# A four-layer graph network: scatter-adding the last layer's expert rows into the output, and moving weights and products at three earlier borders

## The chip, the cores and the metric

The kernel runs on one core of a Trainium2 chip. The metric is device time in microseconds (us) of one execution, the median of the runs; lower is better.

## The reference

A graph of 1250 nodes with 512 features and 21250 edges (sorted by target) passes through four layers. Each layer adds a graph convolution and a linear attention of the normalized features, then a routed feed-forward step:

```python
xn = _layernorm(x)
x = x + gnn(xn, edges) + mix(xn)
x = x + ffn(_layernorm(x))
```

- Layer 0: three GATv2 convolutions, one after another (`m = leaky_relu(xl[src] + xr[dst] + ef)`, softmax of `m @ att` over the edges of a target, weighted sum of `xl[src]`), with `xl = x @ Wl[k]`, `xr = x @ Wr[k]`; a linear attention; 8 experts that choose their nodes.
- Layer 1: two GAT convolutions, a global linear attention (`q`, `k`, `v` by three weights), 8 routed experts and 2 shared ones.
- Layer 2: a convolution with combined bases, linear attention, 10 experts.
- Layer 3: GCN, linear attention, and 32 experts with a capacity, the part that the diff touches most:

```python
probs = softmax(x_flat @ Wg); vals, idx = top_k(probs, 2)
vals = vals / vals.sum(-1)
a = idx.reshape(BTK)                          # BTK = 2500 choices
pos = rank of each choice among those of its expert
keep = pos < C                                # C = 98
dest = where(keep, a * C + pos, N * C)
buf = zeros((N * C, D)).at[dest].set(x_flat[token], mode='drop')
h = relu(einsum('ncd,ndh->nch', buf, W1) + b1)
o = einsum('nch,nhd->ncd', h, W2) + b2
y = segment_sum(o[dest] * (vals * keep), token)
y = where(contrib <= 1e-12, x_flat, y)        # a node that no expert kept
```

All data are float32.

## The kernel before

One class, `Net`, holds the program. Nodes lie in NT = 10 tiles of 128 (the last has 98 rows); `self.x` stays in SBUF. Small helpers do the recurring steps: `weight` (L141, a 1 MB weight by SyncE), `gather` (L231) and `scatter` (L239), both indirect DMAs issued by GpSimd, `evac` (L134, PSUM to SBUF, in turn on ScalarE and VectorE), `feat` (L179, a transposed product), `add_scaled` (L1811). The order on each engine is the program's order as the Tile framework schedules it; `manual_schedule` holds one engine to the written order.

Layer 0's convolutions are `gatv2_fast`. Edges are worked off in groups of four tiles: gathered left rows `xl` (table `tl`, by GpSimd), target fields (`fields`: a broadcast row `nb` and edge attributes, loaded two groups ahead), one-hot matrices (`onehot`, ScalarE), right products of the block (L1286, L1287), scores (`logits`, VectorE, L1299 and L1302), and sums by target (L1353). As a block's targets finish, their nodes' tables for the *next* convolution are made: `gat_tables` (L1154) gives ten closures for a tile, four matmuls with `wl` and `left` (adds the score column, stores to `tl`), then four with `wr` and `right` (splits the value in two, stores to `tr`). They are queued in `late` and run one at a time. `prepare` loads vectors and weights for the convolution after that, from the seventh step on. At the end of a convolution the queues are emptied, and the next starts with `fields(0)`, three `load`s, `fields(1)`, `onehot(0)`.

From layer 0 to layer 1: after the last expert of layer 0 (`layer0_ffn`), 20 gathers bring the expert rows back to their nodes (L231, L1811), the tiles are normalized and transposed, and `global_attention` starts with the weight `wk`; `wv` is loaded when the code comes to it. Between its products stand the steps that count edges per pair of node blocks (L711 matmuls on stored one-hot blocks, `ohb<-oht`, L688).

From layer 2 to layer 3: `tail_steps` gives `need(t)`, which fetches the last two expert rows of a node tile (pipelined over tiles), adds and normalizes. `layer3_attn` calls it tile by tile, beside GCN products (L171). `linear_attention_steps` loads its three weights itself.

Layer 3's feed-forward step, `layer3_ffn`: the router's products and top 2; ranks by matmuls; each node's row is scattered to its places `dest` in the table `routed_in` (20 scatters). The biases b2 and rows of unrouted nodes are added to `self.x`. Then for each of 32 experts: load 98 rows `xe` (ScalarE's queue), transpose (L3164), first product (L179) with ReLU on ScalarE, second product (L3173) into a PSUM bank `y`, evacuate to `o`, store to `routed_out` (ScalarE's queue); two weights are loaded ahead, up to 11 in flight. After the last expert:

```python
for t in range(NT):
    for j in range(2):
        g = tmp.tile([128, D], F32, tag="g", name="g", bufs=4)
        self.gather(g, self.rout[:, :], getI[:, t, j:j + 1])
        self.add_scaled(t, g, w0[:, t, j:j + 1])
    r = rows(t)
    nc.sync.dma_start(self.out[t * 128:t * 128 + r, :], self.x[:r, t, :])
```

Of the kernel before, what the change touches and what calls it, by code (L numbers as in the profile page):

```python
# [16 lines left out]
I32 = mybir.dt.int32  # L17
# [40 lines left out]
class Net:  # L58
# [79 lines left out]
    def weight(self, src, k, n):  # L138

        w = self.wp.tile([128, k, n], F32, tag="w", name="w")  # L140
        self.nc.sync.dma_start(w, src.rearrange("(k p) n -> p k n", p=128))  # L141
        return w
# [591 lines left out]
    def linear_attention_steps(self, xn, xT, w_qkv, w_out, b_out, qscale, finish, added=None,  # L734
                               need=None):
# [14 lines left out]
        with self.tc.tile_pool(name="la", bufs=1) as p, \  # L750
                self.tc.tile_pool(name="latmp", bufs=2) as tmp:
            wk = self.weight(w_qkv[:, D:2 * D], 4, D)
            wv = self.weight(w_qkv[:, 2 * D:3 * D], 4, D)
# [4 lines left out]
            for half in range(2):  # L758
                if half:
                    wq = self.weight(w_qkv[:, 0:D], 4, D)  # L760
                    if qscale != 1.0:
                        nc.scalar.mul(wq, wq, qscale)
# [446 lines left out]
    def gat_layer(self, L, p, xtab, otab, big):  # L1209
# [27 lines left out]
        step = [0]  # L1237

# [16 lines left out]
        def fields(g):  # L1255
            nb = p.tile([128, GE * 128], BF16, tag="nb", name="nb", bufs=4)
            nc.sync.dma_start(nb, self.nbt[g])
            s = p.tile([128, GE * 128], F32R, tag="oh", name="oh", bufs=3)
            nc.sync.dma_start(s[BW:K].bitcast(F32),
                              self.eat[:, g * GE * 128:(g + 1) * GE * 128])  # L1260
            G.setdefault(g, {}).update(nb=nb, s=s)
# [99 lines left out]
        def finish(b):  # L1361
# [44 lines left out]
            def across():  # L1406
# [10 lines left out]
                for t in whole:  # L1417
                    for f in self.gat_tables(nxt, p, t, lambda c, t=t: X[t][:, c, :],
                                             lambda: self.bank("tab", [128, D])):
                        late.append((step[0] + 1, f))  # L1420
# [37 lines left out]
        fields(1)  # L1458
        onehot(0)
        prepared = prepare()  # L1460
        for i in range(FT + 3):
# [9 lines left out]
            if j == 2 and g + 2 < FG:  # L1471
                fields(g + 2)
            if i >= 6 and i % 3 == 0:
                next(prepared, None)
# [19 lines left out]
        bias_cur(NB - 1)  # L1494
        while edge or todo or late:
            for _ in range(2):
                if edge:
                    edge.popleft()[1]()
            for _ in range(2):
                if todo:  # L1500
                    todo.popleft()[1]()
            for _ in range(2):
                if late:
                    late.popleft()[1]()
        return nxt
# [24 lines left out]
    def layer0_ffn_to_layer1_attn(self):  # L1530
# [11 lines left out]
        with self.tc.tile_pool(name="l1a", bufs=1) as p:  # L1542
            xnT = p.tile([128, 4, NP], F32, name="xnT")
            with self.tc.tile_pool(name="l1b", bufs=1) as pb:
                xn = pb.tile([128, NT, D], F32, name="xn")
                with self.weights(), self.psum(3, 2, 3) if fast else self.psum():
                    count_pool()
                    self.counting = self.count_blocks(range(CB), True) if fast else iter(())
                    self.layer0_ffn(xn, xnT)
# [7 lines left out]
                    self.global_attention(xn, xnT, steps)  # L1557
# [91 lines left out]
    def layer0_ffn(self, xn, xnT):  # L1649
# [6 lines left out]
        with self.tc.tile_pool(name="l0f", bufs=1) as p, \  # L1656
# [126 lines left out]
            for t in range(NT):  # L1783
                for j in range(2):
                    g = tmp.tile([128, D], F32, tag="g", name="g", bufs=6)
                    self.gather(g, obuf[:, :], getI[:, t, j:j + 1])
                    self.add_scaled(t, g, G[:, t, j:j + 1])
                self.ready(t)
                self.norm_tile(t, xn[:, t, :])
                self.transpose_tile(xnT[:, :, t * 128:(t + 1) * 128], xn[:, t, :])  # L1790
                self.count(1)
            g1.close()

# [12 lines left out]

    def add_scaled(self, t, psum, gate):
# [6 lines left out]
    def global_attention(self, xn, xnT, steps):  # L1814
# [3 lines left out]
        with self.tc.tile_pool(name="ga", bufs=3) as big, \  # L1818
# [5 lines left out]
            wk = self.weight(I["L1_mix_WkT"], 4, D)  # L1824
# [20 lines left out]
            wv = self.weight(I["L1_mix_WvT"], 4, D)  # L1845
# [531 lines left out]
    def tail_steps(self, xn, xnT):  # L2377
# [22 lines left out]
        def need(t):  # L2400
            with self.tc.manual_schedule(engines={mybir.EngineType.Pool}):
                for u in range(t - n if t == 0 else t, t + 1):
                    for i, f in enumerate(steps):
                        if 0 <= u + n - i < NT:
                            f(u + n - i)
        return need
# [522 lines left out]
    def layer3_attn(self):  # L2929
        nc, I = self.nc, self.I  # L2930
        added = self.both_added()
        with self.tc.tile_pool(name="l3", bufs=1) as p:
            xnT = p.tile([128, 4, NP], F32, name="xnT")
            xn = p.tile([128, NT, D], F32, name="xn")
            need = self.tail_steps(xn, xnT)
# [12 lines left out]
            with self.tc.tile_pool(name="gcn", bufs=2) as tmp:  # L2948
# [3 lines left out]
                else:  # L2952
# [5 lines left out]
                    added)  # L2958
# [77 lines left out]
    def layer3_ffn(self):  # L3036
        nc, I = self.nc, self.I
        NE, ROWS = 32, 32 * CAP
        with self.tc.tile_pool(name="l3f", bufs=1) as p, \
# [15 lines left out]
            xn = p.tile([128, NT, D], F32, name="xn")  # L3055
# [9 lines left out]
            for t in range(NT):  # L3065
                self.norm_tile(t, xn[:, t, :])
# [19 lines left out]
            getI = p.tile([128, NT, 2], I32, name="getI")  # L3086
            G = p.tile([128, NT, NE], F32, name="G")
            with self.tc.tile_pool(name="l3r", bufs=1) as pr1:
# [35 lines left out]
                for t in range(NT):  # L3124
                    r = rows(t)
                    for j in range(2):
                        self.scatter(self.rin, putI[:r, t, j:j + 1], xn[:r, t, :], "moe")
                for j in range(2):
# [4 lines left out]
                nc.vector.tensor_scalar(dest, dest, float(ROWS - 1), None, op0=ALU.min)  # L3133
                nc.vector.tensor_copy(getI, dest)
# [7 lines left out]
                                        op=ALU.mult)  # L3142
                for j in range(2):
# [3 lines left out]
            for t in range(NT):  # L3147
# [7 lines left out]
                self.add_scaled(t, xn[:, t, :], none[:, t:t + 1])  # L3155
            for e in range(NE):
                w1, w2 = ws[2 * e], ws[2 * e + 1]
                er = slice(e * CAP, (e + 1) * CAP)
                xe = tmp.tile([CAP, D], F32, tag="xe", name="xe", bufs=3)
                nc.scalar.dma_start(xe, self.rin[er, :])  # L3160
# [14 lines left out]
                o = tmp.tile([CAP, D], F32, tag="o", name="o")  # L3175
                self.evac(o, y)
                nc.scalar.dma_start(self.rout[er, :], o)
# [4 lines left out]
            for t in range(NT):  # L3182
                for j in range(2):
                    g = tmp.tile([128, D], F32, tag="g", name="g", bufs=4)
                    self.gather(g, self.rout[:, :], getI[:, t, j:j + 1])
                    self.add_scaled(t, g, w0[:, t, j:j + 1])
                r = rows(t)
                nc.sync.dma_start(self.out[t * 128:t * 128 + r, :], self.x[:r, t, :])
# [69 lines left out]
```

## Time and profile before

| | |
|---|---|
| median of 3 runs | 4463.08 us (4459.12 to 4470.91) |
| the profiled execution | 4489.82 us, its span 4487.9 us |
| mean granted TensorE clock | 0.937 |
| instructions | 49486 |
| data moved by DMA | 647.58 MB, mean 144 GB/s |
| last stage: last matmul of an expert ends | 4443.4 us |

The profile is one execution, by the hardware profiler. Times in it are us from the span's start. PE is TensorE, PEld its weight loads, DVE VectorE, ACT ScalarE, POOL GpSimd, SP SyncE; a "q" after an engine is its sequencer or DMA queue. Groups of instructions name line, engine, operation and tile (`out<-in`), count, busy time, mean ns, and the idle time of the engine just before them with what ended most of it. The chain lists the work that ended last, followed back from the end. Stretches give the busy time of each engine in a window, with the granted clock, the mean busy share of the 16 DMA engines and what they moved. Timelines list instructions by start and duration, with the engine's idle time before each in brackets.

### The profile page before, as it was taken

Reading aid. Unit: us, or ns where it says so; the run is one execution under the profiler, and the core shown is the slowest. Engines: PE = TensorE matmul, PEld = TensorE weight load, DVE = VectorE, ACT = ScalarE, POOL = GpSimd, SP = SyncE. Lnnn points to the kernel's source line nnn. Section 1 sums busy time; section 2 is a strip of 40 time slices with the busy share of each in tenths; the row PEclk is TensorE's granted clock in tenths of the full one; section 3 lists DMA queues with packets and bytes.
Section 4 is the critical chain, followed back from the end, with each engine's and each line's share of the span. In section 5 each row is a group of like instructions: output and inputs, shape, how many; then the busy total and the mean of one; then the engine's idle time right before and its main releaser. Section 6 shows DMA issues by size and latency. Waiting matters only on the chain. (4 is left out here: it accounts for less than half of the span.)

```text
span 4487.9 us, 49486 instructions
## 1 busy us (share of the span) xinstructions
PE 3922.2 (87%) x15466; PEld 2415.7 (54%) x15466; DVE 2689.5 (60%) x6338; ACT 1622.8 (36%) x2976; POOL 1351.0 (30%) x1308
## 2 busy tenths in 40 slices
PE   5987998899788867799999999997979896898796
PEld 3434554455354434444788877563546562455474
DVE  5357895888398865523896767314584225687301
ACT  2222442344133375110464446223451232554121
POOL 2017773776466501102000000103131013675102
PEclk9988999999899988899999999999989998997798
DMA  6437664666466423402421110383002653666695
GB/s 220 159 84 211 198 199 150 198 197 193 141 179 189 145 74 108 119 17 64 146 70 42 46 35 29 143 298 128 12 27 83 233 189 119 182 200 199 225 339 181
DMA packets 283001, 647.58 MB, mean 144 GB/s; under 512 B 61673, under 2 KB 108905, under 8 KB 267322
## 3 DMA queue, kind: packets, MB, share of 16 engines
q1 hardware_dynamic: 169290, 357.13, 24.1%
q0 software_dynamic: 73088, 234.75, 18.3%
q10 hardware_dynamic: 40352, 52.44, 3.4%
q8 instruction: 127, 2.08, 0.2%
q14 instruction: 144, 1.18, 0.1%
HBM read 528.87 MB, written 120.65 MB: 145 GB/s over the span
## 5 line engine op out<-in xcount | busy, mean ns | idle before, releaser
L231 POOL DMA_INDIRECT xl<-xl,srcI x564 | 616.8, 1094 | 290.2 <-issue 137.8
L1353 PE MATMUL more<-xl,wT 128*128 128x512 f32 x1128 | 579.7, 601 | 14.5 <-ACT wT L1343 14.0
L1286 PE MATMUL mm<-hl,oh 121*128 121x512 f32 x564 | 419.1, 743 | 73.8 <-DVE s L1299 37.8
L1302 DVE SCALAR_TENSOR_TENSOR junk<-s,att 128x512 f32<-128x512 f32 x534 | 417.9, 783 | 6.8
L1299 DVE TENSOR_TENSOR s<-xl,mm 128x512 f32<-128x512 f32 x534 | 357.8, 679 | 104.0 <-PE mm L1287 48.4
L2129 PE MATMUL more<-hh,e 128*128 128x259 f32 x1600 | 383.7, 385 | 11.7 <-ACT o L2072 8.6
L2129 PEld LDWEIGHTS more<-hh,e 128*128 128x128 f32 x1600 | 295.1, 191 | 75.8 <-issue 17.8
L171 PE MATMUL mm<-w,xnT 128*128 128x512 f32 x640 | 307.8, 620 | 16.6 <-ACT xnT L2388 12.1
L231 POOL DMA_INDIRECT hs<-gcn_h,srcI x188 | 214.6, 1142 | 93.6 <-issue 30.8
L1353 PEld LDWEIGHTS more<-xl,wT 128*128 128x128 f32 x1128 | 196.1, 192 | 74.8 <-issue 27.9
L1287 PE MATMUL mm<-hl,oh 121*128 121x512 f32 x564 | 236.4, 419 | 0.0
L1286 PEld LDWEIGHTS mm<-hl,oh 121*128 121x128 f32 x564 | 111.0, 197 | 215.5 <-issue 117.1
L231 POOL DMA_INDIRECT g<-routed_out,getI x60 | 67.6, 1126 | 488.5 <-DMA routed_out<-o 416.4
L2049 ACT ACTIVATE e<-r,hh 128x512 f32<-128x512 f32 (+1 forms) x240 | 154.2, 646 | 130.7 <-PE more L2129 119.5
L171 PEld LDWEIGHTS mm<-w,xnT 128*128 128x128 f32 x640 | 123.4, 198 | 144.0 <-issue 124.6
L3011 PE MATMUL more<-hl,oh 128*128 128x512 f32 x376 | 161.5, 534 | 30.9 <-DVE oh L2975 10.9
L1273 ACT ACTIVATE oh<-nb 112x512 fp32r<-112x512 bf16 x141 | 88.7, 630 | 273.6 <-DMA nb<-nbt 162.3
L2052 ACT ACTIVATE e<-r,a 128x512 f32<-128x512 f32 (+1 forms) x240 | 152.3, 646 | 71.1 <-DVE e L2054 57.8
L711 PE MATMUL more<-ohs,ohb 128*128 128x512 bf16 x564 | 137.5, 383 | 42.8 <-ACT ohs L695 18.0
L2054 DVE TENSOR_TENSOR e<-e,e 128x512 f32<-128x512 f32 (+1 forms) x240 | 141.5, 596 | 51.2 <-ACT e L2049 44.8
L1287 PEld LDWEIGHTS mm<-hl,oh 121*128 121x128 f32 x564 | 112.4, 199 | 110.1 <-issue 108.4
L1166 PE MATMUL tab<-w,xT 128*128 128x512 f32 x320 | 163.5, 605 | 9.0 <-ACT xT L1415 6.1
(631 smaller groups left out, 7787.8 us busy)
## 6 DMA issues: line engine op xcount, KB each, us to landing
w<-L_ffn_Wp SPq DMA_DIRECT2D x64, 1024.0 KB
w<-L_ffn_table SPq DMA_DIRECT2D x56, 1025.0 KB
neg<-ntab SPq DMA_DIRECT2D x80, 320.0 KB
nb<-nbt SPq DMA_DIRECT2D x141, 128.0 KB
hl<-xr SPq DMA_DIRECT2D x36, 448.0 KB
xr<-tro SPq DMA_DIRECT2D x30, 512.0 KB
xe<-routed_in SPq DMA_DIRECT2D x56, 256.0 KB
routed_out<-o ACTq DMA_DIRECT2D x56, 256.0 KB
```

The costliest lines, as they stand in the source:

```text
L171: self.nc.tensor.matmul(p, lhsT=xT[:, c, t * 128:(t + 1) * 128], rhs=w[:, c, n0:n0 + n], start=c == 0, stop=c == k - 1)
L231: self.nc.gpsimd.indirect_dma_start(out=out, out_offset=None, in_=table, in_offset=bass.IndirectOffsetOnAxis(ap=idx, axis=0), bounds_check ...
L1166: nc.tensor.matmul(d[name], lhsT=xT(c), rhs=L[name][:, c, :], start=c == 0, stop=c == 3)
L1286: nc.tensor.matmul(m, lhsT=s, rhs=hl[:K, 0, :], start=True, stop=False)
L1287: nc.tensor.matmul(m, lhsT=s, rhs=hl[:K, 1, :], start=False, stop=not on_pe(i))
L1299: nc.vector.tensor_tensor(o, d["xl"][:, j, :D], s, op=ALU.add)
L1302: nc.vector.scalar_tensor_tensor(junk, s, 0.0, L["att"], op0=ALU.max, op1=ALU.mult, accum_out=d["lg"][:, j:j + 1])
L1353: nc.tensor.matmul(B[b]["y"], lhsT=d["wT"][:, j, :], rhs=d["xl"][:, j, :D], start=k == 0 and j == 0, stop=last and j == GE - 1)
L2049: nc.scalar.activation(e1[:, :n], R[q, k, 0][:, :n], AF.Exp, bias=HH[q][:, s, 256:257])
L2052: nc.scalar.activation(e2[:, :n], R[q, k, 1][:, :n], AF.Exp, bias=heads[q][0][:, s, 0:1])
L2129: nc.tensor.matmul(ys[j], lhsT=e[:, j * 128:(j + 1) * 128], rhs=HH[q][:, s, :], start=s == 0, stop=s == NT - 1)
L3011: nc.tensor.matmul(y, lhsT=oh, rhs=hl[:, i], start=i + j == 0 and not (self.fast and k), stop=last and i + j == GE)
```

## The change

In layer 3 the node's number travels with its row: `xn` has two more columns, the first holding the number, and rows go to a table of their own, `routed_in3`, that was filled with zeros and numbers of unused rows (1280 and up) before. A table `gates3` holds for each node its first expert and its two gates. Each expert reads the node numbers from its rows, gathers the gates, picks the one that is its own, scales `y` with it on evacuation, and adds its rows to the output in HBM by an indirect DMA with `compute_op=ADD`. `self.x` is stored to the output ahead of the experts. The output has 128 more rows, cut off at the end. Filling the tables with zeros is `clear_places`, called at the start of layer 1's global attention.

In `gatv2_fast` the right products of the last three tiles are left to the next convolution, where they run after `onehot(0)`; fields are loaded three groups ahead instead of two; `prepare` starts at step 15 instead of 6; the closing products use another set of PSUM banks.

Weights: `wk` of layer 1's attention is loaded ahead of the output gathers of layer 0 and `wv` after them, both earlier than its other weights; the three of layer 3's attention after the first call of `need`, which fetches the first node tiles. "Behind" is brought about by a GpSimd memset of one element of the weight's buffer, for which SyncE's load waits.

```diff
-    def weight(self, src, k, n):
+    def weight(self, src, k, n, behind=False):
         w = self.wp.tile([128, k, n], F32, tag="w", name="w")
+        if behind:
+            self.nc.gpsimd.memset(w[:1, 0, :1], 0.0)
         self.nc.sync.dma_start(w, src.rearrange("(k p) n -> p k n", p=128))
...
 (gatv2_fast)
-            nb = p.tile([128, GE * 128], BF16, tag="nb", name="nb", bufs=4)
+            nb = p.tile([128, GE * 128], BF16, tag="nb", name="nb", bufs=5)
-            s = p.tile([128, GE * 128], F32R, tag="oh", name="oh", bufs=3)
+            s = p.tile([128, GE * 128], F32R, tag="oh", name="oh", bufs=4)
...
-                    for f in self.gat_tables(nxt, p, t, lambda c, t=t: X[t][:, c, :],
-                                             lambda: self.bank("tab", [128, D])):
+                    fs = self.gat_tables(nxt, p, t, lambda c, t=t: X[t][:, c, :],
+                                         lambda: self.mm() if ending[0] else
+                                         self.bank("tab", [128, D]))
+                    if t >= NT - 3:
+                        rest.extend(fs[5:])
+                        fs = fs[:5]
+                    for f in fs:
                         late.append((step[0] + 1, f))
...
         fields(1)
+        fields(2)
         onehot(0)
+        for f in L.pop("rest", ()):
+            f()
...
-            if j == 2 and g + 2 < FG:
-                fields(g + 2)
-            if i >= 6 and i % 3 == 0:
+            if j == 2 and g + 3 < FG:
+                fields(g + 3)
+            if i >= 15 and i % 3 == 0:
                 next(prepared, None)
...
 (layer0_ffn)
+            wk = self.weight(I["L1_mix_WkT"], 4, D)
+            with self.tc.manual_schedule(engines={mybir.EngineType.Pool}):
+                for t in range(NT):
...
+                wv = self.weight(I["L1_mix_WvT"], 4, D, behind=True)
...
+    def clear_places(self, p):
+        nc = self.nc
+        self.rin3 = self.dram.tile([32 * CAP, D + 2], F32, name="routed_in3")
+        self.gtab = self.dram.tile([NP + 128, 4], F32, name="gates3")
+        zero = p.tile([128, D + 2], F32, name="zero3")
+        nc.gpsimd.memset(zero, 0.0)
+        nc.sync.dma_start(self.gtab[NP:, :], zero[:, :4])
+        nc.sync.dma_start(self.out[NP:, :], zero[:, :D])
+        nc.gpsimd.iota(zero[:, D:D + 1].bitcast(I32), pattern=[[0, 1]], base=NP,
+                       channel_multiplier=1)
+        for e in range(32):
+            nc.sync.dma_start(self.rin3[e * CAP:(e + 1) * CAP, :], zero[:CAP])
...
 (layer3_attn)
+            def load():
+                ws.extend(self.weight(I["L3_mix_w_qkvT"][:, i:i + D], 4, D, behind=True)
+                          for i in (D, 2 * D, 0))
-            need = self.tail_steps(xn, xnT)
+            need = self.tail_steps(xn, xnT, load)
...
 (layer3_ffn)
-                        self.scatter(self.rin, putI[:r, t, j:j + 1], xn[:r, t, :], "moe")
+                        self.scatter(self.rin3, putI[:r, t, j:j + 1], xn[:r, t, :], "moe")
...
+                nc.vector.tensor_copy(gate[:, :, 1:3], w0)
+                nc.sync.dma_start(self.gtab[:NP, :].rearrange("(t p) c -> p t c", p=128), gate)
...
+                nc.scalar.dma_start(self.out[t * 128:t * 128 + r, :], self.x[:r, t, :])
             for e in range(NE):
-                xe = tmp.tile([CAP, D], F32, tag="xe", name="xe", bufs=3)
-                nc.scalar.dma_start(xe, self.rin[er, :])
+                xe = tmp.tile([CAP, D + 2], F32, tag="xe", name="xe", bufs=4)
+                nc.scalar.dma_start(xe, self.rin3[er, :])
+                to = tmp.tile([CAP, 1], I32, tag="to", name="to", bufs=8)
+                nc.vector.tensor_copy(to, xe[:, D:D + 1].bitcast(I32))
+                g = tmp.tile([CAP, 4], F32, tag="g", name="g", bufs=8)
+                self.gather(g, self.gtab[:, :], to)
+                d = tmp.tile([CAP, 2], F32, tag="d", name="d", bufs=8)
+                nc.vector.tensor_scalar(d[:, :1], g[:, :1], float(e), None, op0=ALU.is_equal)
+                nc.vector.tensor_tensor(d[:, 1:], g[:, 1:2], g[:, 2:3], op=ALU.subtract)
+                nc.vector.scalar_tensor_tensor(d[:, 1:], d[:, :1], d[:, 1:], g[:, 2:3],
+                                               op0=ALU.mult, op1=ALU.add)
...
-                o = tmp.tile([CAP, D], F32, tag="o", name="o")
-                self.evac(o, y)
-                nc.scalar.dma_start(self.rout[er, :], o)
+                o = tmp.tile([CAP, D], F32, tag="o", name="o", bufs=3)
+                nc.vector.tensor_scalar(o, y, d[:, 1:], None, op0=ALU.mult)
+                nc.gpsimd.indirect_dma_start(
+                    out=self.out, out_offset=bass.IndirectOffsetOnAxis(ap=to, axis=0),
+                    in_=o, in_offset=None, bounds_check=NP + 127, oob_is_err=True,
+                    compute_op=ALU.add)
-            for t in range(NT):
-                for j in range(2):
-                    g = tmp.tile([128, D], F32, tag="g", name="g", bufs=4)
-                    self.gather(g, self.rout[:, :], getI[:, t, j:j + 1])
-                    self.add_scaled(t, g, w0[:, t, j:j + 1])
-                r = rows(t)
-                nc.sync.dma_start(self.out[t * 128:t * 128 + r, :], self.x[:r, t, :])
```

## Prediction

> **What bounds the kernel now.** I read the page first (busy time, chain, costliest groups), then the chain of waits over the last 110 us, then the stretches of each stage that the change touches, then the timelines at their borders.
>
> ```profile
> PE 3922.2 (87%) x15466; PEld 2415.7 (54%) x15466; DVE 2689.5 (60%) x6338; ACT 1622.8 (36%) x2976; POOL 1351.0 (30%) x1308
> L231 POOL DMA_INDIRECT g<-routed_out,getI x60 | 67.6, 1126 | 488.5 <-DMA routed_out<-o 416.4
> q1 hardware_dynamic: 169290, 357.13, 24.1%
> q0 software_dynamic: 73088, 234.75, 18.3%
> ```
> TensorE is busy for 87% of the span, so no edit to another engine pays unless TensorE waits there. The change touches five places; in each I look for TensorE's gap. The software queue's packets filled 18.3% of 16 engines for 234.75 MB: 286 GB/s if it ran alone; the hardware queue's, 330 GB/s.
>
> The chain at the end, from the last expert on (start, us, what):
> ```profile
> 4436.44 3.55 PE mm L179 x32
> 4439.99 3.45 PE mm L3173 x8
> 4443.44 0.02 issue
> 4443.46 0.59 ACT o L134
> ...
> 4444.07 2.95 DMA routed_out<-o
> ...
> 4451.97 4.01 DMA g<-routed_out,getI
> ...
> 4476.85 5.24 DMA g<-routed_out,getI
> ...
> 4482.19 0.75 DVE x L1811
> ```
> TensorE's last matmul ends at 4443.4 and the span at 4487.9: 44.5 us of evacuation, store, 20 gathers at one per 1.3 to 1.6 us, the last landing and one output store. The same stage by stretches (us; busy PE, PEld, DVE, ACT, POOL; clock, DMA share, GB/s):
> ```profile
> 4340.00:4380.00 40.00, 40.00 (x246) 28.85 (x244) 2.64 (x5) 10.88 (x28) 0.00 (x0) 1.00 0.96 338
> 4410.00:4444.00 34.00, 33.42 (x188) 22.41 (x186) 1.60 (x3) 9.00 (x23) 0.00 (x0) 1.00 0.09 27
> 4444.00:4488.00 44.00, 0.00 (x0) 0.00 (x0) 15.03 (x20) 0.04 (x1) 22.96 (x20) 0.55 0.59 184
> ```
> The experts are bound by TensorE (40 of 40 us; 7.4 us each, from the chain's 22.2 us per three), but the DMA engines are at 0.96 beside it, and fall idle at about 4408: the weights are some 32 us ahead of their use at the end. Both facts matter below.
>
> At a border of two GATv2 layers (SyncE, then GpSimd, then TensorE):
> ```profile
> 752.31 0.33 SPq L1184 DMA_DIRECT2D xl<-tlo  x1
> ```
> ```profile
> 758.60 1.03 POOL L231 DMA_INDIRECT xl<-xl,srcI  x1 [12.22 <-DMA xl<-tlo]
> ```
> ```profile
> 747.23 3.70 PE L1166 MATMUL tab<-w,xT 128*128 128x512 f32 x8 [0.69 <-ACT xT L1415]
> 752.34 3.70 PE L1166 MATMUL tab<-w,xT 128*128 128x512 f32 x8 [1.41 <-DVE junk L1182]
> 765.70 0.79 PE L1286 MATMUL mm<-hl,oh 121*128 121x512 f32 x1 [9.66 <-DVE s L1299]
> ```
> The next layer's gathers wait for the last left table row; TensorE then waits 9.66 us for edges.
>
> **What the Trainium skill says.** "DMA: Bandwidth & Descriptors", section "Rules for kernel authors", has it that an accumulating DMA reads its destination and writes later with nothing held in between, so each must wait for the earlier one's semaphore: the 32 new adds are a serial chain. Section "Anatomy of one DMA" prices a software DMA at about 2.0 us plus bytes/436e3; the trace's plain scatter of 128 rows lands 2.64 us after GpSimd's instruction, which agrees (2.6). "Collectives: The Full Stack", section "The bandwidth ceiling", says an add needs two source reads, so the read traffic doubles. No accumulate is in the trace of before. "DMA: Bandwidth & Descriptors", section "Issuing engines are not separate DMA queues", says queues share the same engines; the trace agrees, with 0.96 busy while queues of SyncE and ScalarE are both in use.
>
> **Part 1, the end of layer 3.** Removed: the last store to routed_out (2.95), the 20 gathers with their waits, 20 additions, the output stores at the end. In their place the last expert ends with evacuation by VectorE (0.75, the row of its like) and one scatter-add: GpSimd 1.0, landing 3.5 (2.64, plus 0.45 for a second read of 196 KB by the page's price, plus 0.4), then 2.0 to the end (4.96 from the last addition's end to the span's, less 2.95 for the store), 0.2 of small waits: 4443.4 + 0.8 + 1.0 + 3.5 + 2.0 + 0.2 = 4450.9 against 4487.9, **-37.0** (bounds -35 to -38).
>
> What the stage pays for it. Per expert GpSimd gets a gather of 98 rows of 16 bytes and a scatter-add, about 1.0 each; VectorE five instructions, 0.1 to 0.75. Both engines are nearly idle there (0.00 and 2.64 of 40 us), so busy time costs nothing. What can cost is the waits. Each add waits for the one before: its period is 1.0 (GpSimd) + landing. A gather under 0.90 DMA share at 3736.03 was in use 3.5 us after its issue start; a scatter-add has a read more and a write to wait for: 5 to 7 us, taken 6.2, under the 7.4 of an expert. On GpSimd, gathers and adds are paired (two gathers, two adds), so a waiting add holds the next pair's gate gathers, these VectorE's gate arithmetic, and that the evacuation of the next y; by the order of instructions up to about 8 us of landing is hidden. I take +0.05 per expert for the cycle, **+1.6**, and for the first expert, behind ten output stores on ScalarE's queue and the first gate gather, **+0.5** (0 to 2).
>
> DMA traffic: the accumulate reads 6.4 MB more (22 us of 16 engines at 286 GB/s), the 6.4 MB move from ScalarE's queue to the software one (4 us), and there are 32x98 gate packets. The queue's mean packet takes 180 ns (18.3% of 16 x 4487.9 us by 73088); at that the gates cost 35 us of 16 engines, but they are 16 bytes against 3.2 KB, so 1 to 35, taken 10. Together 27 to 61, taken 36, against 32 us of lead and some 10 us of idle share before (0.04 of 240). Cost: 0 to +19; I take **+5**, since the load isn't even. Rows grow from 2048 to 2056 bytes: nothing that the trace prices; bound 0 to 2 in the scatters, which at 1.3 us pace are on the path; taken 0.
>
> **Part 2, the zeros.** SyncE gets 34 stores, 32 of them 98x514 (201 KB): 6.4 MB. They stand behind GpSimd's memset and iota, which stand behind the 20 gathers (to 1844.1), and ahead of the fourth of the count matmuls' inputs:
> ```profile
> 1860.80 14.27 SPq L688 DMA_DIRECT2D ohb<-oht  x4
> ```
> ```profile
> 1872.44 2.28 PE L711 MATMUL more<-ohs,ohb 128*128 128x512 bf16 x12
> ```
> The first of these is the reload when TensorE frees a buffer. In the change SyncE first issues wv and w1 (2.1 MB) and the zeros from about 1848, eight in flight: 8.8 MB at 300 to 340 GB/s last 26 to 29 us, so the fourth input is issued at 1872 and lands at 1876, needed at 1872.4. TensorE is bound from 1860 on (29.93 of 30 us in 1870 to 1900), so this is paid: **+5** (0 to 12). wk ahead of the gathers and wv behind them take 2 MB out of their way: **-1.5** (0 to -3). The manual order of GpSimd's gathers changes nothing that I can see: 0 (0 to +3).
>
> **Part 3, GATv2.** Right products of tiles 7 to 9 leave the layer's end. At the border tile 9's right product already lies behind its left one, so it isn't on the path; those of 7 and 8, two passes of 1.7 us each, lie before it with TensorE full (10 tenths in 700 to 742): -3.4 for each of two borders, -6.8. In the next layer their 5.2 us of TensorE (12 matmuls of 0.43) fall into its 9.66 us wait: 0; without that cover they'd cost 5.2 per border. At the first border the first gather came 6.3 us after the table store's issue, beside 2 MB of weights; at the second, without weights, 3.8 (1180.99 to 1184.78). Weights now come later in the layer: -2.5. Fields fetched three groups ahead, and more buffers: ScalarE's wait for nb is on an idle engine, 0, but in the first groups of each of three layers up to 5: -1.7. Sum **-11** (-4 to -18).
>
> **Part 4, into layer 3.** Three 1 MB weights move behind the first fetches. Before, they are issued 3724.13 to 3726.3 together with the GCN weight:
> ```profile
> 3736.03 1.05 POOL L231 DMA_INDIRECT g<-routed_out,getI  x1 [54.80 <-DVE oh L2975]
> ```
> The last expert's store is issued at 3729.0 and the first gather starts 7.0 us later, with DMA at 0.93 in 3728 to 3740; in the last stage the same wait is 3.5. TensorE does nothing from 3728.3 to 3756, so the 3.5 are on the path: -3.5, +0.5 for three memsets ahead of gathers on GpSimd: **-3** (0 to -6). The first weight is needed at 3812 and would be there by 3775: cover of 37 us.
>
> **The sum.** -37.0 + 1.6 + 0.5 + 5 + 5 - 1.5 - 11 - 3 = -40.4. The profiled execution took 4489.8 (span 4487.9, 1.9 around it); it lies 26.7 above the median of 4463.1, so I take the difference from the median: **4423**.
>
> **Rivals.** (a) *The chain of scatter-adds becomes the bound; slower than before.* Place: GpSimd's waiting add, each expert. For it: the read-modify-write waits for two trips to memory under 0.96 busy engines, and no row of before shows one. Against: the gather's 3.5 under 0.90. From a period of 7.4 on, 32 experts pay 32 x (period - 7.4); at 8.7 the whole gain of 40 is gone. At 10 it is +83, and 4506; at 9.2, +58, and about 4480.
> (b) *DMA becomes the bound of the last stage.* Traffic of 61 us at the upper end against 42 of lead and idle share, or the packets of a read-modify-write costing twice: weights late by 20 to 30 us more. For it: 0.96. Against: they are idle for 34 us at the end. 4443 to 4453, say 4447.
> (c) *The early parts give nothing*: the zeros cost 12, GATv2's gap merely moves to the edges' first scores. -37 + 7 + 12 - 1.5 - 3 = -22.5, so 4441.
> (d) *The stage costs nothing and GATv2 pays in full*: -37 + 2 + 3.5 - 18 - 6 = -55.5, so 4408.
>
> **How the numbers follow.** Forecast (4412 to 4432): 0.42. (d) 0.12, (c) 0.14, (b) 0.15, (a) 0.17, of which about a quarter ends between 4450 and 4476. 0.3% is 13.4 us, what a measurement of this kernel can tell from no change: faster is below 4449.7, slower above 4476.5. Faster: 0.42 + 0.12 + 0.14 + 0.09 of (b) = 0.77. Same: 0.06 of (b), 0.04 of (a) = 0.10. Slower: 0.13. The range leaves out a little of (d) and most of (a): 4400 to 4472.
>
> **What would show it.** Part 1: no gather of routed_out after the last L179; an end 6 to 8 us after the last matmul; tp to tp still 7.4 us per expert with TensorE at 40 of 40. If the chain bounds (rival a), TensorE's gaps stand at y's evacuation and GpSimd's adds lie more than 7.4 apart, each released by the DMA of the one before. If DMA bounds (b), TensorE waits for w, late in the stage. Part 2: a gap on TensorE before the fourth group of L711, released by ohb. Part 3: the gap before the first L1286 shrinks from 9.66, and the first gather comes under 4 us after the last tlo store. Part 4: first gather 3.5 us after the last store. I am wrong if scatter-adds land in more than 7 us under load, or if the read-modify-write takes more of the engines than its bytes.

## The result, and the profile after

| | median, us | runs |
|---|---|---|
| before | 4466.99 | 4459.12 to 4477.33, 4 runs |
| changed | 4522.78 | 4519.89 to 4526.84, 4 runs |

The ratio is 1.0124, with an interval of 1.0100 to 1.0149: 56 us slower, where 40 us faster was forecast. The profiled execution of the changed kernel is one of its four runs and has a span of 4518.6 us; that of the kernel before (4489.8 us) is none of the runs in this table.

Where it went is seen if the last stage is cut at the same marks in both profiles: GpSimd's first scatter to `routed_in`, the first transpose of an expert, the end of the last expert product, the end of the span.

| us | before | changed |
|---|---|---|
| first scatter to first transpose | 30.1 | 31.0 |
| the 32 experts | 240.2 | 352.8 |
| from the last product to the end | 44.5 | 10.8 |
| the stage | 314.9 | 394.7 |

The tail is shorter by 33.7, nearly as forecast, and the experts are longer by 112.6: 11.0 us each on average instead of 7.5. The group of the first expert product in the changed kernel's page (count, busy and mean, then the idle time before it):

```profile
L181 PE MATMUL mm<-xT,w 128*128 128x98 f32 x1024 | 137.7, 296 | 73.5 <-DVE o L3243 71.7
```
TensorE waits for `o`, the evacuation of y, which is now VectorE's alone. The same stretch that had 40.00 us of TensorE in 40 before, and 0.96 of the DMA engines:

```profile
4340.00:4380.00 40.00, 29.89 (x154) 20.72 (x152) 5.83 (x20) 5.42 (x15) 10.03 (x8) 0.83 0.65 209
```
VectorE is busy for 5.83 us of 40, the DMA engines for 0.65. Nothing is full; something waits. The cycle of two experts, engine by engine in the changed kernel's timeline. TensorE transposes two experts, then stands still:

```profile
4331.73 0.84 PE L3231 MATMUL tp<-ident,xe 98*128 98x98 f32 x8
...
4348.09 2.02 PE L181 MATMUL mm<-xT,w 128*128 128x98 f32 x8 [5.30 <-DVE o L3243]
...
4355.51 0.84 PE L3231 MATMUL tp<-ident,xe 98*128 98x98 f32 x8
```
ScalarE's queue reloads two of the four `xe` buffers as soon as the transposes have read them:

```profile
4332.45 0.80 ACTq L3217 DMA_DIRECT2D xe<-routed_in  x2
```
VectorE copies the node numbers of those rows (6 us later, when they have landed), computes gates (again 6 us later), and only then evacuates a y:

```profile
4339.07 0.15 DVE L3220 COPY to<-xe 98x1 int32<-98x1 int32 x1 [5.92 <-DMA xe<-routed_in]
...
4345.27 0.15 DVE L3224 TENSOR_SCALAR d<-g 98x1 f32<-98x1 f32 x1 [5.30 <-DMA g<-gates,to]
...
4346.90 0.15 DVE L3224 TENSOR_SCALAR d<-g 98x1 f32<-98x1 f32 x1 [1.16 <-DMA g<-gates,to]
...
4347.29 0.74 DVE L3243 TENSOR_SCALAR o<-mm,d 98x512 f32<-98x512 f32 x1
```
and GpSimd's gather of the gates lies between:

```profile
4339.53 1.09 POOL L233 DMA_INDIRECT g<-gates,to  x1 [5.02 <-DVE to L3220]
```
By the order of instructions on VectorE, the rows and gates in these lines are those of experts 19 and 20 (counted from 0), and the y's of experts 15 and 16 stand behind them. So work for four experts later, which isn't urgent, blocks the one that TensorE needs. 7.3 us from the transposes to the reloaded rows, 8.2 to both experts' gates and the evacuation's start, 0.8 for it, 7.4 of TensorE's work to the next transposes: 23.8 between the two lines above.

What GpSimd's 32 gathers of gates and 32 scatter-adds waited for (us in all, times; two of five lines):

```profile
  DVE o L3243: 196.0, 32
...
  DMA out<-o,to: 2.5, 7
```
All 32 waits for `o` are the adds'. The seven for an add's landing are gathers'; no add waited for the one before. So the chain of adds, the rival that ended on the slower side, is not what held this kernel.

The two profiles also differ before the last stage: the changed kernel gets to its first scatter 49 us earlier (4124.0 against 4173.1), 33 of them in the GATv2 layers and 12 in layer 3. No other profile of the same code shows this, as the first experiment tells.

### The profile page after: what moved, and what is told of

The parts are those of the page before. It is cut to its first block, busy times and chain, and to the rows that moved or that the text cites. A ratio compares the mean times of both kernels' runs of the same rounds, so it can differ in the third digit from the quotient of the medians.

```text
span 4518.6 us, 49692 instructions
## 1 busy us (share of the span) xinstructions
PE 3930.3 (87%) x15448; PEld 2420.8 (54%) x15466; DVE 2706.3 (60%) x6464; ACT 1609.8 (36%) x2960; POOL 1406.5 (31%) x1360
## 5 line engine op out<-in xcount | busy, mean ns | idle before, releaser
L1294 PE MATMUL mm<-hl,oh 121*128 121x512 f32 x564 | 413.9, 734 | 29.6 <-DVE s L1307 14.9
L173 PE MATMUL mm<-w,xnT 128*128 128x512 f32 x640 | 303.5, 612 | 12.8 <-ACT xnT L2426 8.1
L1295 PE MATMUL mm<-hl,oh 121*128 121x512 f32 x564 | 228.4, 405 | 0.0
L181 PE MATMUL mm<-xT,w 128*128 128x98 f32 x1024 | 137.7, 296 | 73.5 <-DVE o L3243 71.7
L181 PEld LDWEIGHTS mm<-xT,w 128*128 128x128 f32 x1024 | 132.0, 209 | 88.0 <-DVE o L3243 73.9
L2030 PE MATMUL mm<-w,xnT 128*128 128x258 f32 x640 | 158.5, 391 | 5.2 <-DVE junk L2014 4.6
```

Source lines behind the costliest of these rows:

```text
L173: self.nc.tensor.matmul(p, lhsT=xT[:, c, t * 128:(t + 1) * 128], rhs=w[:, c, n0:n0 + n], start=c == 0, stop=c == k - 1)
L181: self.nc.tensor.matmul(p, lhsT=w[:, c, f * 128:(f + 1) * 128], rhs=xT[:, c, s:s + n], start=c == 0, stop=c == k - 1)
L1294: nc.tensor.matmul(m, lhsT=s, rhs=hl[:K, 0, :], start=True, stop=False)
L1295: nc.tensor.matmul(m, lhsT=s, rhs=hl[:K, 1, :], start=False, stop=not on_pe(i))
L2030: nc.tensor.matmul(m, lhsT=chunk(layer, c)[:, t * 128:(t + 1) * 128], rhs=w[:, c, :], start=c == 0, stop=c == k - 1)
```

## The experiments

The kernel before was run again beside each group of experiments and read 4494 to 4506 us there, so each kernel is given as a ratio to the runs of before beside it (95% interval in brackets), and stages are compared by length.

**The early parts alone.** The changed kernel with the `layer3_ffn` of before.

```diff
-            self.clear_places(p1)
...
-                nc.vector.tensor_scalar(o, y, d[:, 1:], None, op0=ALU.mult)
-                nc.gpsimd.indirect_dma_start(
...
+                self.evac(o, y)
+                nc.scalar.dma_start(self.rout[er, :], o)
```


> Leaves out of the change the part in layer 3's experts and the zeros; GATv2, the weights of layer 1 and of layer 3 are as changed. If the two profiles are taken as they stand, the changed kernel reaches the last stage's scatters 49 us earlier (4124.0 against 4173.1); but the profile of before lies 27 us above its median, so the gain is between 21 and 49 us: 4418 to 4446. By the predicted steps (-11, -1.5, -3) it would be 15.5: 4451.

Measured 0.9983 (0.9972 to 0.9994), 8 us faster: the 21 to 49 us were not there. In this kernel's profile the last gather of layer 0's convolutions comes at 1541 us from the span's start. In the eight other kernels below with the same GATv2 code it comes at 1529 to 1539, in the three without it at 1538 to 1541, and in the profile of the changed kernel alone at 1504.

**The experts' part alone.** The kernel before with the `layer3_ffn`, the longer output and the zeros of the changed one.

```diff
+            self.clear_places(p1)
...
-                self.evac(o, y)
-                nc.scalar.dma_start(self.rout[er, :], o)
+                nc.vector.tensor_scalar(o, y, d[:, 1:], None, op0=ALU.mult)
+                nc.gpsimd.indirect_dma_start(
...
```


> Only the part in layer 3's experts with its zeros, on the kernel before. The changed kernel is 56 slower in all; with early parts that gain 21 to 49, this part costs 77 to 105: 4544 to 4572, with 11.5 us per expert instead of 7.4 as in the changed kernel's profile. If instead the early parts gain only 15, it is 4538.

1.0183 (1.0150 to 1.0216), 82 us slower; experts 350.6 us. The whole loss lies here, and more than the whole.

**The order on VectorE.** The changed kernel with the experts' loop written as a pipeline, in which the transposes also come one expert ahead. The edit in short (bounds left out, comments added):

```diff
+            with self.tc.manual_schedule(engines={mybir.EngineType.DVE, mybir.EngineType.Pool}):
...
+                for e in range(NE):
...
+                    fetch(e + 3)                      # xe
+                    turn(e + 1)                       # transposes, xT
...
                     nc.vector.tensor_scalar(o, y, S[e]["d"][:, 1:], None, op0=ALU.mult)
+                    gates(e + 1)                      # the three operations on d
+                    place(e + 2)                      # to, and the gather of the gates
                     nc.gpsimd.indirect_dma_start(
...
```


> The changed kernel with the experts' loop written as a pipeline and VectorE and GpSimd held to it: the node numbers and gate gather of an expert come two experts ahead, its gate arithmetic one ahead, each behind the evacuation of y; the same instructions and DMAs. Theory 1 (the evacuation stands in VectorE's queue behind the gates of four experts later, which wait for the reload of xe and for the gather): 7.4 to 7.8 us per expert, 120 us less, 4400. Theory 2 (the chain of scatter-adds is slow by itself): 11.5 per expert stays, 4520. Theory 3 (the DMA engines bound the stage): at least 9 us per expert, over 4445.

0.9979 (0.9962 to 0.9996). The same instructions and transfers in another order take 271.1 us for the experts instead of 352.8: 82 us were the order. But 8.47 per expert is not 7.5: between theory 1 and theory 2. What the adds wait for now:

```profile
  DMA out<-o,to: 140.8, 28
```
With VectorE's queue out of the way the chain of adds comes to the front. Some of them in a row:

```profile
4317.08 1.52 POOL L3274 DMA_INDIRECT out<-o,to  x1 [6.83 <-DMA out<-o,to]
...
4325.21 1.53 POOL L3274 DMA_INDIRECT out<-o,to  x1 [5.23 <-DMA out<-o,to]
...
4337.45 1.52 POOL L3274 DMA_INDIRECT out<-o,to  x1 [9.34 <-DMA out<-o,to]
```
8 to 12 us from one to the next, each of these released by the one before.

**More buffers for the rows.**

```diff
-                xe = tmp.tile([CAP, D + 2], F32, tag="xe", name="xe", bufs=4)
+                xe = tmp.tile([CAP, D + 2], F32, tag="xe", name="xe", bufs=8)
```


> The changed kernel with 8 buffers instead of 4 for xe, nothing else. Theory 1: the reload (7 us of the 23 us cycle of two experts) leaves the cycle, the gather stays in VectorE's queue: 8 to 9 us per expert, 4410 to 4445. Theories 2 and 3: 11.5 us per expert stays, 4515 to 4530.

1.0164 (1.0130 to 1.0198), experts 349.1: no gain, against what theory 1 in its narrow form expected. VectorE's timeline in this kernel:

```profile
4365.23 0.15 DVE L3220 COPY to<-xe 98x1 int32<-98x1 int32 x1 [5.38 <-DMA out<-o,to]
4372.17 0.15 DVE L3224 TENSOR_SCALAR d<-g 98x1 f32<-98x1 f32 x1 [6.78 <-DMA g<-gates,to]
...
4372.56 0.74 DVE L3243 TENSOR_SCALAR o<-mm,d 98x512 f32<-98x512 f32 x1
```
With rows at hand the scheduler puts `to` still further ahead, seven experts, where it has to wait for its own buffer (one of 8), and that is free only when an add has landed. The queue is the same, another wait stands in it. So theory 1 holds as "the evacuation stands behind work for later experts, and waits for whatever that waits for"; the reload of xe is only one such wait.

**No gather for the gates.**

```diff
+                nc.vector.tensor_reduce(xn[:, :, D + 1], prod, AX.X, ALU.add)   # first expert
+                nc.vector.tensor_copy(xn[:, :, D + 2:], w0)                      # its two gates
...
-                self.gather(g, self.gtab[:, :], to)
+                g = xe[:, D + 1:]
```


> The changed kernel, but the first expert and the two gates travel in the row beside the node number (516 columns), so that the gates table and its 32 gathers go; the order is the scheduler's again. If the gather is what made VectorE's queue late, the cycle of 11.5 us per expert loses its 6 to 7 us of gather in each pair: 8 to 9 per expert, the run at 1.000 to 1.003 of the kernel before. If the chain of scatter-adds bounds by itself, 11.5 stays (1.012).

1.0003 (0.9992 to 1.0014); experts 281.1 us, 8.79 each, as expected if the gather made the queue late. The order is the scheduler's, and the evacuations still stand behind later experts' rows, but with one landing in the queue instead of two. It and the written order take away much the same 72 to 82 us by different means, so these aren't added up.

**What makes the adds slow.** Two variants of the written order, one run each. The first leaves out the sum, the second the weights after the first ten.

```diff
-                        in_=o, in_offset=None, bounds_check=NP + 127, oob_is_err=True,
-                        compute_op=ALU.add)
+                        in_=o, in_offset=None, bounds_check=NP + 127, oob_is_err=True)
```


> The kernel with the written order, with a plain indirect write in place of the add (leaves out the sum: a node keeps one of its rows). In the written order two adds were 7.4 to 10 us apart, each released by the one before. If the second read of the add makes it slow, the writes land 2 us earlier and the stage is TensorE's again at 7.4 us per expert, 30 us less. If the load on the DMA engines does, the writes land about as late, and the stage stays within 10 us of the written order's 314.

```diff
-                    w1, w2 = ws[2 * e], ws[2 * e + 1]
+                    w1, w2 = ws[2 * e % 10], ws[2 * e % 10 + 1]
...
-                            load(ahead)
```


> The kernel with the written order, without the weights' loads after the first 11: experts use the first ten over and over (leaves out the other weights). If the load on the DMA engines makes the adds slow, they land in 3.5 to 4.5 us after GpSimd and the stage is TensorE's at 7.4 us per expert; if the read-modify-write is slow by itself, 6 us or more of landing stay.

Experts 242.2 and 241.7 us, 7.6 each: TensorE's pace with either change. The same stretch in the first and in the second:

```profile
4300.00:4340.00 40.00, 40.00 (x241) 28.36 (x240) 7.32 (x28) 8.86 (x25) 11.83 (x12) 1.00 0.95 338
```
```profile
4300.00:4340.00 40.00, 40.00 (x240) 28.21 (x239) 8.03 (x33) 8.32 (x24) 12.97 (x10) 1.00 0.31 56
```
The slow period takes both, the add and the load: an add without the load, or a plain write under a load of 0.95, keeps up. The plain write's GpSimd instruction took 1.01 us, the add's 1.52. The trace's DMA packets differ too: the 98 rows of an add are 98 packets of 2 KB, 1.6 us of 16 engines in all, those of a plain write 56 packets, most of 4 KB, and 0.65 us (both after the weights were in). Why the load delays the add's packets so much more isn't shown.

**Letting the adds fall behind.** Gates in the row, the written order, 8 buffers for `o` and 16 for `to`, so that VectorE needs no add to have landed until eight are open.

```diff
-                to = tmp.tile([CAP, 1], I32, tag="to", name="to", bufs=8)
+                to = tmp.tile([CAP, 1], I32, tag="to", name="to", bufs=16)
...
-                    o = tmp.tile([CAP, D], F32, tag="o", name="o", bufs=3)
+                    o = tmp.tile([CAP, D], F32, tag="o", name="o", bufs=8)
```

> Gates in the row, the written order, and 8 buffers for o (16 for the places), so that VectorE doesn't wait for an add until 8 are open. If the adds' own chain is slower than 7.4 us per expert (8 to 9), TensorE is not held, and the last adds come some 20 us after the last matmul less what they catch up once the weights are in: 0.990 to 0.996 of the kernel before. If DMA bandwidth bounds, TensorE waits for weights and it is 0.997 or more.

0.9960 (0.9945 to 0.9975), 18 us faster than before, 8 of which the early parts give. TensorE takes 239.2 us for the experts, and the tail is 32.0 instead of 10.8. GpSimd's adds, some under load and some after the weights were in:

```profile
4306.54 1.53 POOL L3267 DMA_INDIRECT out<-o,to  x1 [7.80 <-DMA out<-o,to]
4314.37 1.51 POOL L3267 DMA_INDIRECT out<-o,to  x1 [6.30 <-DMA out<-o,to]
```
```profile
4431.99 1.50 POOL L3267 DMA_INDIRECT out<-o,to  x1 [3.72 <-DMA out<-o,to]
4437.14 1.51 POOL L3267 DMA_INDIRECT out<-o,to  x1 [3.65 <-DMA out<-o,to]
```
The chain of waits gives the landings, counted from the start of GpSimd's instruction:

```profile
4392.04 9.78 DMA out<-o,to
4402.64 7.56 DMA out<-o,to
4416.22 4.53 DMA out<-o,to
4437.14 4.76 DMA out<-o,to
```
Here the chain runs nearly by itself, so its period can be read: from 4214.7 to 4411.0 there are 21 adds, 9.35 us each on average (the first two come at TensorE's pace); afterwards 5.2 each, of which 1.5 on GpSimd, about 2.9 from there to the landing and 0.8 until GpSimd starts the next. At 9.35 it loses 1.9 us per expert to TensorE, and gets back a part at the end. The DMA share in 4300 to 4340 is 0.99 and TensorE is busy for 40.00 us of 40: with the traffic of the adds in, the weights still come in time.

**The early parts one by one.** The GATv2 part, and the weights of layer 3's attention, each on the kernel before. (The first expectation counts from a mark 10.5 us ahead of the span's start.)

```diff
+                    if t >= NT - 3:
+                        rest.extend(fs[5:])
+                        fs = fs[:5]
...
+        fields(2)
         onehot(0)
+        for f in L.pop("rest", ()):
+            f()
```


> Only the GATv2 part of the change, on the kernel before. By the prediction -11 us (0.9975, bounds 0.996 to 0.999). By the profiles of five kernels with this part against two without (last gather of layer 0's convolutions ends at 1547 to 1552 us against 1548 and 1549, though the first gather after the second border comes 5 us earlier) it gains nothing: 0.999 to 1.001.

0.9997 (0.9982 to 1.0013): nothing.

```diff
-            need = self.tail_steps(xn, xnT)
+            need = self.tail_steps(xn, xnT, load)
```


> Only the three weights of layer 3's attention behind the first fetches, on the kernel before. By the prediction -3 us (0 to -6); by the profiles all of the early parts' 8 us: 0.998 to 0.9985. If the early parts' gain lies in GATv2 instead, 0.9993.

0.9987 (0.9973 to 1.0002): 6 us if it is taken at its middle, which just can't be told from none by itself; the 8 us of the early parts together can.

Why GATv2 gives nothing: the gain at the border is there. First gather after the second border in a profile without this part (experts' part alone) and with it (early parts alone):

```profile
1190.50 1.02 POOL L231 DMA_INDIRECT xl<-xl,srcI  x1 [12.67 <-PE tab L1166]
```
```profile
1185.19 1.04 POOL L233 DMA_INDIRECT xl<-xl,srcI  x1 [12.44 <-DMA xl<-tlo]
```
The firmer measure is from the last gather of one convolution to the first of the next. It is 78 to 82 us in the three profiles without this part, and in the nine with it, the changed kernel's apart, 75 to 77 at the first border and 71 to 73 at the second. TensorE's wait before the first right product (9.66 in the kernel before) is gone. But then, with this part, TensorE and VectorE wait where they did not:

```profile
1215.27 0.80 PE L1294 MATMUL mm<-hl,oh 121*128 121x512 f32 x1 [4.71 <-issue]
...
1223.00 0.79 PE L1294 MATMUL mm<-hl,oh 121*128 121x512 f32 x1 [6.50 <-issue]
```
VectorE's waits at 1214.5 and 1221.6 (7.2 and 5.7 us) end with signals from outside the engines. From the first gather to the last matmul by the identity (L1289, then L1297), which only the first groups of a convolution have, it is 39 to 47 us without this part and 48 to 54 with it: the lead is gone.

The changed kernel's own profile is the exception. It has the same border, then 33 us for that stretch, and none of VectorE's waits up to 1500 us ends with such a signal; they total 42 to 54 us in the nine other profiles with this part and 20 to 36 in the three without. That is where most of its 33 us lie, and it is the one profile in which the gain at the border stays. What the signals are (landings of gathers or of fields) the profile doesn't name, so it stays open why they came in time there, and whether the kernel before would gain as much in such an execution.

**Plain writes to two tables.** An expert's row for a node goes to one table if it is the node's first choice and to another if it is the second; no two rows meet, so no scatter waits. After the last expert the tables are read straight.

```diff
+        self.sums = self.dram.tile([2 * NP, D], F32, name="sums")
...
+                nc.vector.tensor_scalar(d, xe[:, D + 1:], float(e), float(NP),
+                                        op0=ALU.not_equal, op1=ALU.mult)
+                nc.vector.tensor_tensor(to, d, xe[:, D:D + 1], op=ALU.add)
...
+                    self.scatter(self.sums, S[e]["to"], o, "moesum")
...
+                    (nc.sync, nc.scalar)[j].dma_start(
+                        g, self.sums[j * NP + t * 128:j * NP + (t + 1) * 128, :])
                     self.add_scaled(t, g, w0[:, t, j:j + 1])
```


> The changed kernel without adds: each expert's rows go by plain scatters to two tables by node, one for a node's first choice and one for its second (no two rows meet, so no scatter waits for another); after the last expert 20 plain loads on two queues take the place of the 20 gathers, and VectorE scales and adds as before. The tables are filled with zeros in layer 1 (5.2 MB more). If waiting for each other's read-modify-write under load is what the adds cost, the experts stay at 7.35 us and the tail is 5 us to the last landing, 15 to 17 us for 5.1 MB, 6 to the end, 26 instead of 44.5: 0.993 to 0.995 of the kernel before. If plain scatters wait under the load too, 0.998 or more.

0.9958 (0.9946 to 0.9970), 19 us faster than before, a little less than expected. Experts 238.1 us; the tail is 30.3 where 26 was expected, and the stretch of layer 1 with the zeros takes 312 us, where the kernels with fewer zeros take 304 to 307. At the end the DMA engines are nearly full while TensorE and GpSimd have nothing to do, so most of this tail is transfer:

```profile
4460.00:4482.00 22.00, 0.00 (x0) 0.00 (x0) 13.89 (x20) 0.00 (x0) 0.00 (x0) 0.50 0.87 314
```

This and the version with open adds both beat the kernel before and the changed one, with 8 us of the early parts in either; between the two the intervals don't tell.

## Why the prediction was wrong

**The step that failed** is the sentence of part 1 on the pairs: "a waiting add holds the next pair's gate gathers, these VectorE's gate arithmetic, and that the evacuation of the next y; by the order of instructions up to about 8 us of landing is hidden. I take +0.05 per expert for the cycle". The order was read rightly, with the evacuation behind the gates, but only the add's landing was followed through it. Two landings stand in it that have nothing to do with the add: the reload of `xe`, which can't begin before this pair's transposes, and the gather of the gates, which can't begin before that. In the cycle shown above they take 7.3 us and most of 8.2. The price was +1.6; written in another order, the loop is 82 us shorter, of the 112.6 that the experts had got longer.

**The add's period** was taken as 7.2 (1.0 on GpSimd and 6.2 to land), just under an expert's 7.4. It is 9.35 under load and 5.2 without. For the unloaded one 1.0 and 3.5 were taken; it is 1.5 on GpSimd and 2.9 to land, so the landing came at about the right time after the start, 4.2 to 4.8 us, but by luck. The 2.64 us of the plain scatter, from which the 3.5 were made, are counted from the start of GpSimd's instruction and not from its end. Counted that way, the price in the Trainium skill's "DMA: Bandwidth & Descriptors", section "Anatomy of one DMA", gives an estimate of 2.9 for two reads of 196 KB, well short of the add's 4.2 to 4.8. The 0.8 until the next add starts was left out. Under load the landing was bounded by a gather that was in use 3.5 us after its issue; the 0.90 beside it is the share of 3730 to 3740, and in the gather's own 4 us the share was 0.75. Plain writes at 0.95 keep TensorE's pace, but the add doesn't. The rival on the slower side put its price on this and was near it: at 9.2 it said 32 x 1.8 = 58 us. It gave about the right time, for a cause that in the changed kernel stood behind the other one: no add waited for the one before.

**The DMA engines**: +5 for late weights was not needed. They are at 0.99 in the version with open adds, and TensorE has no gap. That version has no gathers of gates, but the variant with plain writes has them, and TensorE has no gap there either. So rival (b) held for neither part of the traffic; both at once at TensorE's pace no run shows. One of the signs named for being wrong did come: an add takes 1.6 us of 16 engines and a plain write of the same bytes 0.65. (Moving 6.4 MB to the other queue is 3 us at the two rates given, not 4; nothing hangs on it.)

**The tail** was -37.0 and is -33.7: the add takes 1.51 us of GpSimd, not 1.0, and from its end to the end of the span there are 8.2 us, not 5.5. The mechanism was right. The time that was left out is in GpSimd's drain at the end, 6.0 us long, which is over at 4517.8, 3.7 us after SyncE's last wait; in the kernel before, with GpSimd's work done earlier, a drain of 5.4 us was over a microsecond before SyncE's last wait.

**The zeros** were to stop TensorE for 5 us ahead of the fourth group of count matmuls. SyncE's queue was held as forecast:

```profile
1818.96 22.23 SPq L1843 DMA_DIRECT2D routed_in<-zero  x32
1841.29 10.74 SPq L690 DMA_DIRECT2D ohb<-oht  x4
```
but TensorE shows no wait for it: products stand at that place (L181, 44 matmuls from 1833.5 to 1849.6), and the count matmuls come after. From the first output gather to the first tile of layer 1's convolution it is 304.5 to 306.7 us in the seven kernels with the zeros and the early weights, the changed one among them. It is 304.6 with the early weights but no zeros, 303.7 with the zeros alone, and 299.9, 303.5 and 304.3 in three that have neither. So the zeros cost 0 to 2 us beside the early weights, not 5, and the early weights gain nothing that shows, against -1.5.

**GATv2** was -11 and is 0 (-8 to +6 by the interval). The gain at the two borders came, about 5 and 7 us on average, and is given back within 50 us. The -2.5 of the later weights isn't in it: from the left table's store to the first gather at the first border it is 6.6 to 7.3 us with this part and 6.3 to 7.7 without, not 3.8. The step that named the next layer's wait as a cover for the moved products, and what follows on it, did not ask what bounds that layer's first 50 us; TensorE isn't it (31.6 of 50 us busy in 1190 to 1240 without this part, 29.6 with it).

**Into layer 3** was -3: the wait from the last expert's store to the first gather is 3.0 instead of 7.0 (3734.45 to 3737.47 in the early parts' profile), -4, and the measured 6 and 8 us are in keeping with that or somewhat more.

```profile
3737.47 1.05 POOL L233 DMA_INDIRECT g<-routed_out,getI  x1 [51.76 <-DVE oh L3005]
```

**What isn't closed**: the experts' part alone cost 82 us (67 to 97) and the early parts gave 8 (3 to 13), which makes 74, and the whole change measured 56 (45 to 67), beside other runs of the kernel before. The intervals overlap, so this may be noise. But the profile of the whole change has a stage 80 us longer and is 49 us faster ahead of it, most of that in two stretches with many gathers: GATv2, and layer 3, whose 188 gathers of `hs` take 283 us instead of 294 to 301 in the kernel before and in the first three experiments. The kernel before was faster, too, beside those runs: 4467 us, against 4494 to 4506 beside the experiments. There is no profile of it from among them, so how much of the 49 us the change gave and how much was common to both kernels stays open.

## What to carry to other kernels

On an engine that works in order, ask of each small instruction added not how long it takes but what it waits for, and what urgent one stands behind it: work of 0.15 us for four experts later cost 2.6 us per expert here (82 us over 32 experts), with VectorE busy for 15% of the time. More buffers didn't help here, where the scheduler used them to put such work still further ahead; an order that puts the urgent instruction first did. And a chain of DMAs that wait for each other is priced by its period under the load that it will meet, best from a run of that operation itself.

## What was not expected of the hardware

An indirect scatter-add of 98 rows of 2 KB took 1.51 us of GpSimd and landed about 2.9 us after that with the DMA engines at about 0.3, and the next began 0.8 us later. At a share of 0.99 the adds came every 9.35 us, while plain scatters of the same rows at 0.95 kept up with 7.35 us per expert. An add kept the 16 DMA engines busy for 1.6 us and a plain scatter for 0.65. A gather of 98 rows of 16 bytes cost GpSimd 1.09 us, and VectorE waited until 4.7 us after its end, at a share of 0.65.
